# Gathers with a limit on the index: the slots of neighbouring node tiles are left out

## The chip, the cores and the metric

The kernel runs on one core of one Trainium2 chip. The time is the device time of one execution in microseconds (us), as the median of several. Before the change it is 2587.53 us, the median of 8 runs between 2582.63 and 2596.87 us.

A core has five engines with queues of their own: PE (matrix products; its weight loads are listed as PEld), DVE (vector work), ACT (activations), POOL (here above all the issuer of gathers) and SP (issuer of plain DMAs). Sixteen DMA engines move the data for all queues.

## The reference

Two graph attention layers (GAT) with normalisation and residuals, over 3,125 nodes with 768 features and 53,125 edges. The edges are 25,000 random pairs in both directions and one self loop per node, sorted by destination. The layer adds a second self loop for each node.

```python
h = relu(layernorm(x))
# layer 1: 4 heads of 256; layer 2: one head of 768
xl = (x @ W).reshape(n, heads, out_ch)
alpha_src = einsum('nhc,hc->nh', xl, a_src);  alpha_dst = einsum('nhc,hc->nh', xl, a_dst)
e = leaky_relu(alpha_src[src] + alpha_dst[dst], 0.2)
m = segment_max(e, dst);  e = exp(e - m[dst]);  s = segment_sum(e, dst)
alpha = e / (s[dst] + 1e-16)
out = segment_sum(xl[src] * alpha[:, :, None], dst) + bias
# then layer norm (layer 1 also relu), plus a dense residual of the layer's input
```

At the end `x` is added. All data are float32.

## The kernel before

The program has two parts: `in_order`, written for edges sorted by destination, and `any_order`, a general part that runs only if a flag says that the edges don't suit the first one. With these inputs only `in_order` does work.

`in_order` cuts the nodes into 25 tiles (`NB`) of 125 nodes (`P`). Since the edges are sorted, the edges of a tile lie together. For each tile the kernel takes a window of fixed size: `J` = 18 columns of 128 slots, 2,304 edges, from the first edge of the tile on (for the last tile the window is moved back so that it ends with the list). A tile has about 2,125 edges, so a window also holds edges of the neighbouring tile: at its end, or for the last tile at its beginning. A slot is column `j`, partition `p`; its number among all is `c = b * J + j`.

The stages in order of time:

1. `edge_list` (L188) reads the edge list and counts where each tile begins. `windows` (L236) loads each tile's window, turns it so that slots lie on partitions, and makes three tables of 128 x 450: `rel_s` (L259), the destination minus the tile's first node, so 0 to 124 for the tile's own edges; `idx_s` (L262), the source node as an integer, which is the row that a gather reads; and `hi_s` (L264), the source's tile. All of this is DVE work behind loads of SP. `keep` (L268) marks neighbouring slots with the same destination and is stored to memory four times by SP.
2. `softmax` (L327) for layer 1 finds the attention weight `al` of every slot with one-hot products. It works on all slots, foreign ones too, and gives them finite weights.
3. The dense product `x @ W1` (L588) writes `table1`, 3,125 rows of 1,024 floats.
4. `sums` (L460) for layer 1, the first of the two gather stages, described below. Between its columns run the steps of `end1` (normalisation and the dense product into `table2`, L655 to L683) and the dense residual (L624).
5. `softmax` and 13 of 25 residual tiles (L717) for layer 2, then `sums` for layer 2 on `table2`, with rows of 768 floats, with the rest of the residual between its columns and `end2` (L748 to L753) for the result.

In `sums`, for each tile and each column, POOL issues one indirect DMA (L477), which reads 128 rows of the table, one for each index in column `c` of `idx_s`, into a buffer `g` (10 buffers in layer 1, 13 in layer 2). DVE makes the one-hot matrix `oh` (L488) from `rel_s`: a slot whose `rel_s` lies outside 0 to 124 has a zero in all 125 columns that are used. For most columns ACT multiplies the rows with the weight into `hi`, rounded (L495), DVE forms what is left in `g` itself (L496), and PE adds both into the tile's sum `pa` (L500). For the other columns (2 of 18 in layer 1, 5 of 18 in layer 2) the weight is put into the one-hot matrix (L507, L510) and one float32 product (L512) is made. So a foreign slot's row is read, weighted and multiplied, and a zero column takes it out of the sum. Once per tile POOL gathers `ao` (L483), 128 rows of 2 or 5 floats with the weight of the self loop, which DVE compares at L518.

A gather can be issued when its buffer is free, that is when PE (and DVE) have used the buffer's last content. The order of instructions on each engine is set by a planner, which simulates the engines with a cost for each instruction and picks by the order of the program text; so POOL's place for `ao` among the gathers changes from tile to tile. Each engine then runs its queue in order.

Of the kernel before, what the change touches and what calls it, by code (L numbers as in the profile page):

```python
# [9 lines left out]
F32 = mybir.dt.float32  # L10
# [5 lines left out]
OP = mybir.AluOpType  # L16
# [10 lines left out]
J = 18  # L27
# [29 lines left out]
def in_order(  # L57
# [16 lines left out]
    nc = tc.nc  # L74
    N, D = x.shape
# [4 lines left out]
    P = 125  # L80
    NB = N // P
# [37 lines left out]
    rel_s = const.tile([128, NB * J], F32, name="rel_s")  # L119
    idx_s = const.tile([128, NB * J], I32, name="idx_s")  # L120
# [9 lines left out]
    def load_rows(q, t, src_, b):  # L130


        if b < NB - 1:
            q.dma_start(t, src_[b * P:b * P + 128, :])
        else:
            q.dma_start(t[:112], src_[b * P:b * P + 112, :])
            q.dma_start(t[112:P], src_[b * P + 112:(b + 1) * P, :])
# [29 lines left out]
    def start_of(b):  # L167
        return nc.values_load(starts[0:1, b:b + 1], engines=[SP], min_val=0, max_val=E - S)
# [67 lines left out]
    def windows(pe):  # L236

        per = 126 // J
        with tc.tile_pool(name="wn", bufs=1) as ep:
            k16 = ep.tile([NB, S], I16, name="k16")  # L240
            src_s = ep.tile([128, NB * J], F32, name="src_s")
            for b0 in range(0, NB, per):
                n = min(per, NB - b0)
                wd = ep.tile([128, 128], I32, name="wd", bufs=2)
                ws = ep.tile([128, 128], I32, name="ws", bufs=2)
                for k in range(n):
                    st = start_of(b0 + k)
                    nc.sync.dma_start(wd[k * J:(k + 1) * J, :],
                                      dst[ds(st, S)].rearrange("(j p) -> j p", p=128))
                    nc.sync.dma_start(ws[k * J:(k + 1) * J, :],  # L250
                                      src[ds(st, S)].rearrange("(j p) -> j p", p=128))
                    nc.sync.dma_start(k16[b0 + k:b0 + k + 1, :], dst16_d[ds(st, S)][None, :])
                for t, to in ((wd, dst_s), (ws, src_s)):
                    tf = ep.tile([128, 128], F32, name="tf", bufs=2)
                    nc.vector.tensor_copy(tf[:n * J, :], t[:n * J, :])
                    pt = pe.tile([128, 512], F32, name="pe")
                    nc.tensor.transpose(pt[:, :n * J], tf[:n * J, :], ident[:n * J, :n * J])
                    nc.vector.tensor_copy(to[:, b0 * J:(b0 + n) * J], pt[:, :n * J])
            nc.vector.tensor_tensor(rel_s.rearrange("p (b j) -> p b j", j=J),  # L259
                                    dst_s.rearrange("p (b j) -> p b j", j=J),  # L260
                                    base_f[:, :, None].to_broadcast([128, NB, J]), OP.subtract)
            nc.vector.tensor_copy(idx_s, src_s)  # L262
            q, _ = divided(ep, src_s, [128, NB * J], "sh")
            nc.vector.tensor_copy(hi_s, q)  # L264

            keep = ep.tile([NB, S + 2], BF16, name="keep")
            nc.vector.memset(keep, 0.0)
            nc.vector.tensor_tensor(keep[:, 1:S], k16[:, 1:], k16[:, :S - 1], OP.is_equal)  # L268
            for h in range(H):
                nc.sync.dma_start(keep_d[h * NB:(h + 1) * NB, :], keep)  # L270
# [189 lines left out]
    def sums(heads, cols, table, al, alo_d, bias, split, ahead, gp, pp, end, more=iter(())):  # L460


        width = heads * cols
        f = width // 2
        n = min(cols, f)
        todo = iter(())
        for b in range(NB):
            own = gp.tile([128, width], F32, name="own", bufs=2)
            pa = pp.tile([P, 2, 512], F32, name="pa", bufs=2)
            ao = gp.tile([128, heads + 1], F32, name="ao", bufs=2)  # L470
            for i in range(2):
                nc.tensor.matmul(pa[:, i, :f], ones_r, bias[:, i * f:(i + 1) * f], start=True, stop=False)
            for j in range(J):
                c = b * J + j
                g = gp.tile([128, width], F32R, name="g", bufs=ahead)
                gf = g.bitcast(F32)
                nc.gpsimd.indirect_dma_start(  # L477
                    out=gf, out_offset=None, in_=table[:, :],
                    in_offset=bass.IndirectOffsetOnAxis(ap=idx_s[:, c:c + 1], axis=0))
                if j == 6:  # L480
                    load_rows(nc.sync, own, table, b)
                if j == 2:
                    nc.gpsimd.indirect_dma_start(  # L483
                        out=ao, out_offset=None, in_=alo_d[:, :],
                        in_offset=bass.IndirectOffsetOnAxis(ap=at_last[:, b:b + 1], axis=0))
                if split(j) or heads > 1:
                    oh = gp.tile([128, 128], F32R, name="oh", bufs=8)
                    nc.vector.tensor_scalar(oh, iota_f, rel_s[:, c:c + 1], None, op0=OP.is_equal)  # L488
                if split(j):

                    hi = gp.tile([128, width], F32R, name="hi", bufs=4)
                    for h in range(heads):
                        cs = slice(h * cols, (h + 1) * cols)
                        a = al[:, j, h, b:b + 1]
                        nc.scalar.activation(hi[:, cs], gf[:, cs], AF.Copy, scale=a)  # L495
                        nc.vector.scalar_tensor_tensor(g[:, cs], gf[:, cs], a, hi[:, cs].bitcast(F32),  # L496
                                                       op0=OP.mult, op1=OP.subtract)
                    for t in (hi, g):
                        for i in range(2):
                            nc.tensor.matmul(pa[:, i, :f], oh[:, :P], t[:, i * f:(i + 1) * f],  # L500
                                             start=False, stop=(j == J - 1 and t is g))
                else:
                    w = gp.tile([128, heads, P], F32, name="w", bufs=4)
                    for h in range(heads):
                        a = al[:, j, h, b:b + 1]
                        if heads == 1:
                            nc.vector.tensor_scalar(w[:, h, :], iota_f[:, :P], rel_s[:, c:c + 1], a,  # L507
                                                    op0=OP.is_equal, op1=OP.mult)
                        else:
                            nc.scalar.activation(w[:, h, :], oh[:, :P].bitcast(F32), AF.Copy, scale=a)  # L510
                    for o in range(0, width, n):
                        nc.tensor.matmul(pa[:, o // f, o % f:o % f + n], w[:, o // cols, :], gf[:, o:o + n],  # L512
                                         start=False, stop=(j == J - 1 and (o + n) % f == 0))
                next(todo, None)
                next(more, None)

            iso = gp.tile([P, 1], F32, name="iso", bufs=2)
            nc.vector.tensor_tensor(iso, ao[:P, heads:], node_f[:P, b:b + 1], OP.not_equal)  # L518
            aw = gp.tile([P, heads], F32, name="aw", bufs=2)
            nc.vector.tensor_scalar(aw, ao[:P, :heads], iso, None, op0=OP.max)  # L520
            z = gp.tile([P, width], F32, name="z", bufs=2)
            for o in range(0, width, n):
                nc.vector.scalar_tensor_tensor(z[:, o:o + n], own[:P, o:o + n], aw[:, o // cols:o // cols + 1],
                                               pa[:, o // f, o % f:o % f + n], op0=OP.mult, op1=OP.add)
            for _ in todo:
                pass
            todo = end(b, z)
            next(todo)
        for _ in todo:
            pass  # L530


    with tc.tile_pool(name="m1", bufs=1) as mp:
        al1 = mp.tile([128, J, H, NB], F32, name="al1")
        with tc.tile_pool(name="w1", bufs=1) as wp, tc.tile_pool(name="pm1", bufs=1, space=PSUM) as pm1:
# [5 lines left out]
            with tc.tile_pool(name="d1", bufs=2) as dp, tc.tile_pool(name="pd1", bufs=1, space=PSUM) as pp:  # L541
# [15 lines left out]
                for _ in fold(dp, abs1, w1, NK1, H, C1, wa1, True):  # L557
                    pass
                windows(pp)
                for b in range(NB):  # L560
                    gi, o = b // GB, (b % GB) * P
# [34 lines left out]
        with tc.tile_pool(name="w2", bufs=1) as wp, tc.tile_pool(name="g1", bufs=1) as gp, \  # L596
# [53 lines left out]
            def end1(b, z):  # L650
# [33 lines left out]
                store_rows(nc.sync, table2, b, row)  # L684

            sums(H, C1, table1, al1, alo1_d, b1_r, lambda j: j % 9 != 4, 10, gp, pp, end1, later())


# [540 lines left out]
```

## Time and profile before

| | |
|---|---|
| median of 8 runs | 2587.53 us |
| profiled execution | 2584.87 us |
| its span | 2583.1 us |
| PE busy | 2271.8 us (88%) |
| DVE busy | 1889.5 us (73%) |
| ACT busy | 1311.4 us (51%) |
| POOL busy | 1300.6 us (50%) |
| moved by DMA | 638.09 MB, of which 420.88 MB by POOL's queue |
| gathers (L477) | 900, mean 1314 ns on POOL, 6.0 us from issue to landing (median) |
| TensorE clock granted | 0.938 of full speed (mean) |

The page of the profile gives the busy time of each engine over the whole span; a window query gives the same for a stretch of time. In a group's line stand the source line, the engine, the operation, the tiles written and read, the count, the busy time, the mean duration, and the idle time ahead of it with what ended it. A wait's line gives who waited for whom: total us, number of times, longest one. The busy time of a DMA instruction on POOL is the time in which POOL makes the transfer, not the transfer itself.

The stages by time: edge list and windows to about 170 us, softmax and dense product of layer 1 to about 520 us, gathers of layer 1 from about 520 to 1570 us, softmax of layer 2 and the first residual tiles to about 1900 us, gathers of layer 2 from 1791 us to the end, most of them after 1890 us.

### The profile page before, as it was taken

What the parts mean: (1) busy time and instruction counts of PE and PEld (TensorE: products, weight loads), DVE (VectorE), ACT (ScalarE), POOL (GpSimd) and SP (SyncE); (2) the same over time, 40 slices, a digit from 0 to 9 for tenths busy, and PEclk for the clock granted to TensorE, in tenths of its full rate; (3) what the DMA queues carried; (4) which work ended last, traced back from release to release, by engine and by line L of the source; (5) the groups of instructions that cost most, each with busy time, mean ns of one, the idle gap of its engine ahead of it and who ended that gap; (6) DMA issues with size and microseconds to landing.
All of it is one profiled execution on the core that took longest, in us unless ns stands there. A gap on an engine that the chain in (4) does not pass through costs nothing.

```text
span 2583.1 us, 35850 instructions
## 1 busy us (share of the span) xinstructions
PE 2271.8 (88%) x11226; PEld 1493.7 (58%) x11226; DVE 1889.5 (73%) x4289; ACT 1311.4 (51%) x2834; POOL 1300.6 (50%) x1007
## 2 busy tenths in 40 slices
PE   0969999939999999999999998768998898899776
PEld 0846654415666666666666675554566666566554
DVE  3559996026888989888898997685166777677886
ACT  5313321115887878788887995001033444444443
POOL 5100000037667667666676772002057778787775
PEclk9989999969999999999999998767999999999898
DMA  4228721176889888888888996873268998888887
GB/s 153 85 86 295 252 95 58 48 251 231 285 288 314 294 313 314 278 326 291 314 308 281 329 331 219 287 278 106 69 219 289 316 311 294 273 290 284 295 295 235
DMA packets 185428, 638.09 MB, mean 247 GB/s; under 512 B 31215, under 2 KB 50036, under 8 KB 184334
## 3 DMA queue, kind: packets, MB, share of 16 engines
q0 software_dynamic: 104032, 420.88, 47.8%
q1 hardware_dynamic: 76484, 202.08, 22.5%
q10 hardware_dynamic: 4714, 12.75, 1.4%
q8 instruction: 92, 1.51, 0.2%
q14 instruction: 106, 0.87, 0.1%
HBM read 566.11 MB, written 69.49 MB: 246 GB/s over the span
## 4 chain that ended last, share of the span: by engine, by line
PE 60%; DMA 10%; DVE 8%; issue 4%; POOL 2%; ACT 2%; SPq 1%; DVEq 0%; ACTq 0%; POOLq 0%
PE pa L500 19%; PE p L677 10%; PE pr L717 8%; PE pr L624 8%; PE pa L512 7%; DMA g<-table,idx_s 6%; PE pm L588 5%; DVE g L496 3%; DMA ao<-alo_d,at_last 2%; PE pq L377 1%; ACT hi L495 1%; POOL at L294 1%; PE p L664 1%; POOL g L477 1%; PE pr L713 1%
## 5 line engine op out<-in xcount | busy, mean ns | idle before, releaser
L477 POOL DMA_INDIRECT g<-table,idx_s x900 | 1182.8, 1314 | 1136.3 <-DVE oh L488 417.6
L495 ACT ACTIVATE hi<-g,al 128x256 fp32r<-128x256 f32 (+1 forms) x1925 | 970.7, 576 | 588.5 <-PE pa L500 281.7
L496 DVE SCALAR_TENSOR_TENSOR g<-g,al,hi 128x256 fp32r<-128x256 f32 (+1 forms) x1925 | 988.3, 566 | 116.6 <-ACT hi L495 110.9
L500 PE MATMUL pa<-hi,oh 128*125 128x512 f32 (+1 forms) x1450 | 580.0, 481 | 12.6 <-ACT hi L495 7.1
L500 PE MATMUL pa<-g,oh 128*125 128x512 f32 (+1 forms) x1450 | 457.8, 393 | 51.5 <-DVE g L496 50.4
L500 PEld LDWEIGHTS pa<-hi,oh 128*125 128x125 f32 x1450 | 269.4, 193 | 187.1 <-ACT hi L495 67.1
L500 PEld LDWEIGHTS pa<-g,oh 128*125 128x125 f32 x1450 | 268.3, 192 | 128.3 <-DVE g L496 86.5
L717 PE MATMUL pr<-wr,h 128*125 128x384 f32 x800 | 303.4, 518 | 0.0
L624 PE MATMUL pr<-h0k,wr 128*128 128x500 f32 (+1 forms) x672 | 299.0, 542 | 0.4 <-DMA h0k<-h0T_d 0.4
L677 PE MATMUL p<-w,h1T 128*125 128x384 f32 (+1 forms) x800 | 296.8, 490 | 1.8 <-DVE h1T L668 1.8
L512 PE MATMUL pa<-g,w 128*125 128x384 f32 (+1 forms) x900 | 288.8, 453 | 4.5 <-ACT w L510 3.7
L588 PE MATMUL pm<-w,h 128*125 128x512 f32 x600 | 275.5, 607 | 0.0
L512 PEld LDWEIGHTS pa<-g,w 128*125 128x125 f32 x900 | 170.3, 193 | 84.2 <-issue 25.7
L488 DVE TENSOR_SCALAR oh<-iota_f,rel_s 128x128 fp32r<-128x128 f32 x775 | 200.3, 288 | 21.1 <-PE pa L500 20.1
L717 PEld LDWEIGHTS pr<-wr,h 128*125 128x125 f32 x800 | 155.4, 199 | 94.0 <-issue 19.4
L677 PEld LDWEIGHTS p<-w,h1T 128*125 128x125 f32 x800 | 150.6, 189 | 73.5 <-issue 3.0
L588 PEld LDWEIGHTS pm<-w,h 128*125 128x125 f32 x600 | 110.0, 191 | 118.9 <-issue 118.9
L624 PEld LDWEIGHTS pr<-h0k,wr 128*128 128x128 f32 x672 | 124.2, 191 | 66.0 <-issue 22.5
L377 PE MATMUL pq<-tabs,ohs 125*128 125x100 bf16 (+1 forms) x2700 | 111.4, 199 | 42.2 <-DVE ohs L365 40.6
L377 PEld LDWEIGHTS <-ohs 125*128 125x128 bf16 x2700 | 106.2, 103 | 59.8 <-DVE ohs L365 53.1
L518 DVE TENSOR_TENSOR iso<-ao,node_f 125x1 f32<-125x1 f32 x50 | 7.8, 157 | 161.7 <-DMA ao<-alo_d,at_last 161.7
L590 ACT ACTIVATE row<-pm 125x512 f32<-125x512 f32 x50 | 29.7, 597 | 169.9 <-PE pm L588 159.8
(173 smaller groups left out, 1717.2 us busy)
## 6 DMA issues: line engine op xcount, KB each, us to landing
bd<-dst_d SPq DMA_DIRECT2D x50, 576.0 KB
bs<-slo_d SPq DMA_DIRECT2D x50, 576.0 KB
g<-table,idx_s POOLq DMA_INDIRECT x900, 6.0
r1T_d<-rt SPq DMA_DIRECT2D x100, 125.0 KB
r1t<-r1T_d SPq DMA_DIRECT2D x25, 500.0 KB
h1T_d<-h1T SPq DMA_DIRECT2D x25, 500.0 KB
h<-h1T_d SPq DMA_DIRECT2D x25, 500.0 KB
own<-table SPq DMA_DIRECT2D x24, 512.0 KB
```

What stands on the lines that cost most here:

```text
L377: nc.tensor.matmul(q[:, j], ohs[:P, (j0 + j) * 128:(j0 + j + 1) * 128], tabs[:, i], start=(i == 0), stop=(i == 2))
L477: nc.gpsimd.indirect_dma_start(out=gf, out_offset=None, in_=table[:, :], in_offset=bass.IndirectOffsetOnAxis(ap=idx_s[:, c:c + 1], axis=0))
L488: nc.vector.tensor_scalar(oh, iota_f, rel_s[:, c:c + 1], None, op0=OP.is_equal)
L495: nc.scalar.activation(hi[:, cs], gf[:, cs], AF.Copy, scale=a)
L496: nc.vector.scalar_tensor_tensor(g[:, cs], gf[:, cs], a, hi[:, cs].bitcast(F32), op0=OP.mult, op1=OP.subtract)
L500: nc.tensor.matmul(pa[:, i, :f], oh[:, :P], t[:, i * f:(i + 1) * f], start=False, stop=(j == J - 1 and t is g))
L512: nc.tensor.matmul(pa[:, o // f, o % f:o % f + n], w[:, o // cols, :], gf[:, o:o + n], start=False, stop=(j == J - 1 and (o + n) % f == 0))
L588: nc.tensor.matmul(pm, h0[gi][:, k, o:o + P], w1[:, k, i * 512:(i + 1) * 512], start=(k == 0), stop=(k == NK1 - 1))
L590: nc.scalar.activation(row[:, i * 512:(i + 1) * 512], pm, AF.Copy)
L624: nc.tensor.matmul(pm[:, :nb * P], wr1[:, k, m * 128:(m + 1) * 128], loaded[gi, k][:, :nb * P], start=(k == 0), stop=(k == NK1 - 1))
L677: nc.tensor.matmul(pm[:, :n], hT[:, k, :], w2[:, k, o:o + n], start=(k == 0), stop=(k == NK2 - 1))
L717: nc.tensor.matmul(pm[:, :384], h1[:, k, :], wr2[:, k, i * 384:(i + 1) * 384], start=False, stop=(k == NK2 - 1))
```

## The change

In `windows`, DVE marks the slots whose `rel_s` is below 0 or at least 125, except for those of tile 0 (the first 18 columns), and adds `N` = 3,125 to their index; these indices then lie past the table's last row, 3,124. In `sums`, each gather is given that last row as a limit, with the note that an index beyond it is no error (before, the instruction carried the table's 3,125 rows as its limit, and an index beyond it would have been an error): rows with such an index are not read, and their place in the buffer keeps what it held before. Tile 0 still reads every slot, and its 18 columns go through all 10 or 13 buffers, so that every buffer holds numbers from then on. What the skipped places hold is weighted and multiplied as before and meets the zero column of the one-hot matrix. The gathers of `ao` (L483) are not touched.

```diff
@@ windows
             nc.vector.tensor_tensor(rel_s.rearrange("p (b j) -> p b j", j=J),
                                     dst_s.rearrange("p (b j) -> p b j", j=J),
                                     base_f[:, :, None].to_broadcast([128, NB, J]), OP.subtract)
-            nc.vector.tensor_copy(idx_s, src_s)
+            away = ep.tile([128, NB * J], F32, name="away")
+            nc.vector.tensor_scalar(away, rel_s, 0.0, float(N), op0=OP.is_lt, op1=OP.mult)
+            past = ep.tile([128, NB * J], F32, name="past")
+            nc.vector.tensor_scalar(past, rel_s, float(P), float(N), op0=OP.is_ge, op1=OP.mult)
+            nc.vector.tensor_add(away, away, past)
+            nc.vector.memset(away[:, :J], 0.0)
+            nc.vector.tensor_add(away, away, src_s)
+            nc.vector.tensor_copy(idx_s, away)
             q, _ = divided(ep, src_s, [128, NB * J], "sh")
             nc.vector.tensor_copy(hi_s, q)
@@ sums
                 nc.gpsimd.indirect_dma_start(
                     out=gf, out_offset=None, in_=table[:, :],
-                    in_offset=bass.IndirectOffsetOnAxis(ap=idx_s[:, c:c + 1], axis=0))
+                    in_offset=bass.IndirectOffsetOnAxis(ap=idx_s[:, c:c + 1], axis=0),
+                    bounds_check=N - 1, oob_is_err=False)
```

## The prediction

> **What bounds the kernel now.** I read first the busy times of the page, then the windows by stage, then POOL's waits and its timeline in the two gather stages, and last the rows of the operations that the change touches.
>
> ```profile
> span 2583.1 us, 35850 instructions
> PE 2271.8 (88%) x11226; PEld 1493.7 (58%) x11226; DVE 1889.5 (73%) x4289; ACT 1311.4 (51%) x2834; POOL 1300.6 (50%) x1007
> DMA packets 185428, 638.09 MB, mean 247 GB/s; under 512 B 31215, under 2 KB 50036, under 8 KB 184334
> ```
>
> PE looks like the bound and POOL half idle. These are averages, so I cut the span by stage (the columns are busy us and instruction counts of PE, PE's weight loads, DVE, ACT, POOL, then PE's clock, the DMA share and GB/s):
>
> ```profile
> core 0: us, PE busy (x) PEld busy (x) DVE busy (x) ACT busy (x) POOL busy (x), PEclk, DMA share, GB/s
> 600.00:1437.00 837.00, 826.61 (x2975) 540.91 (x2975) 711.98 (x1977) 689.42 (x1751) 565.91 (x395) 0.99 0.87 300
> 1792.00:1900.00 108.00, 103.72 (x317) 58.65 (x315) 25.28 (x53) 9.97 (x11) 26.48 (x26) 0.95 0.36 119
> 1900.00:2100.00 200.00, 183.23 (x705) 130.31 (x704) 151.57 (x297) 87.83 (x101) 159.75 (x133) 0.96 0.89 303
> 2100.00:2300.00 200.00, 180.94 (x684) 126.99 (x683) 148.17 (x297) 85.04 (x99) 159.78 (x133) 0.94 0.86 289
> 2420.00:2520.00 100.00, 79.11 (x293) 52.87 (x292) 81.56 (x166) 46.68 (x54) 78.67 (x71) 0.93 0.89 301
> ```
>
> Then what POOL waits for: in layer 1 (600 to 1437 us) the first line below, in layer 2 (1900 us to the end) the second, and, of POOL's timeline in layer 2, four issues.
>
> ```profile
> POOL g L477 <- PE pa L500: 204.0, 205, 4.3
> ...
> POOL g L477 <- PE pa L500: 39.3, 129, 0.3
> ...
> 2216.53 0.94 POOL L483 DMA_INDIRECT ao<-alo_d,at_last  x1 [0.30 <-issue]
> 2217.77 0.94 POOL L477 DMA_INDIRECT g<-table,idx_s  x1 [0.30 <-issue]
> 2219.02 0.95 POOL L477 DMA_INDIRECT g<-table,idx_s  x1 [0.30 <-issue]
> 2220.27 0.94 POOL L477 DMA_INDIRECT g<-table,idx_s  x1 [0.30 <-DMA g<-table,idx_s]
> ```
>
> The reader is to see two different stages. In layer 1, PE is busy 826.6 of 837 us and POOL waits for PE to free gather buffers, up to 4.3 us at a time. POOL needs 565.9 + 395 x 0.30 (the gap ahead of every issue) = 684 us of 837, so it has 153 us over, 0.39 us per issue. In layer 2, from 1900 us on, the longest wait of POOL for anything is 0.3 us, which is the fixed gap: 159.78 + 133 x 0.30 = 199.7 us of 200. There POOL issues gathers back to back, and its pace sets the end; 450 of the layer's 475 indirect DMAs are issued that way (the 1792 to 1900 window holds about 25). PE (181 of 200 us) and the DMA engines (0.86) come next.
>
> **The change part by part.** How many rows drop out follows from the seeded edge list: a window has 2,304 slots, a node tile about 2,125 edges. In tiles 1 to 24, 4,300 slots of 55,296 are foreign. They lie at the window's end: per layer 23 gathers become wholly empty (mostly slot column 17) and 23 partly. That is 4,300 / 128 = 33.6 gathers' worth of rows, 4,300 x 4,096 B = 17.6 MB in layer 1 and 4,300 x 3,072 B = 13.2 MB in layer 2, 4.8% of the 638 MB.
>
> *New DVE work in windows().* Two compares, two adds and a memset join; the cast to integers only changes its input. The nearest rows, at the same 128x450 and lower down at another size:
>
> ```profile
> L181 DVE TENSOR_SCALAR shu<-sht 128x450 f32<-128x450 f32 x1 | 0.4, 397 | 0.0
> L182 DVE TENSOR_TENSOR shq<-shq,shu 128x450 f32<-128x450 f32 x1 | 0.6, 628 | 0.0
> L109 DVE MEMSET eps<- 128x1 f32 x1 | 0.1, 59 | 0.7 <-PEq L1215 0.7
> ```
>
> 2 x 0.40 + 2 x 0.63 + 0.06 = 2.1 us. They run once, near 162 us. Behind them on DVE stand the division that makes hi_s, the keep mask, and so SP's stores of keep and the first loads of bd behind those. DVE then idles 1.2 us for the keep store and 1.5 us for bd. If these transfers are not moved by the delay, the idle time swallows all of it; if they are, the whole softmax of layer 1 starts 2.1 us later. Ends 0 and +2.1; keep is made after the new instructions in program order, so part of it passes through: I take +1.
>
> *The gathers' bytes.* PE, DVE and ACT still work through every slot, with the buffer's old rows under a zero one-hot column, so nothing there shrinks. What shrinks is transfer time. In layer 1 it is covered by PE. In layer 2 it would be worth 13.2 MB / 0.289 MB per us = 46 us if the transfers set the pace; but POOL's issue is never held by a landing there (no wait over 0.3 us). A gather that lands earlier only makes ACT's next wait for POOL start earlier. I take 0; ends -46 and 0. The Trainium skill, in "DMA: Bandwidth & Descriptors", section "Anatomy of one DMA — SWDGE (gpsimd) path", gives a software-issued DMA a fixed part and a part that goes with bytes over 436 GB/s. By that rule the layer-2 saving would be an estimated 30 us, and the total 2558 us; the rule has no term for an issuing engine that is the bound.
>
> *POOL's time for one gather.* This is the term that decides, since 450 of them stand in a row: each 0.1 us is 45 us in layer 2, and in layer 1 only what exceeds 0.39 us counts. The rows:
>
> ```profile
> L477 POOL DMA_INDIRECT g<-table,idx_s x900 | 1182.8, 1314 | 1136.3 <-DVE oh L488 417.6 <-PE pa L500 308.4 <-DMA h<-h1T_d 221.6
> L483 POOL DMA_INDIRECT ao<-alo_d,at_last x50 | 49.7, 995 | 30.6 <-DVE iso L518 12.8 <-issue 9.8 <-DVE aw L520 4.4
> L134 POOL DMA_DIRECT2D xt<-in_x_dram x19 | 10.8, 573 | 38.9 <-DVE bn_mv L315 12.0 <-DVE bn_st L313 10.9 <-DMA ws<-in_src_dram 6.5
> ```
>
> An undisturbed gather takes 0.94 us whether its rows have 3,072 B or, for ao in layer 2, 8 B: the price goes with the instruction and its 128 indices, not with what is moved. What lies over 0.94 falls together with DVE's two-input instructions of L496. A plain DMA over 128 rows costs 0.57 us, so handling 128 indices is worth at most 0.94 - 0.57 = 0.37 us. No row has a gather with a limit that skips. Ends for an ordinary gather: 0, if the comparison is part of the price already (the gather of before already carries the table's 3,125 rows as a limit, past which an index would be an error), and +0.37, if every index is handled once more: 450 x 0.37 = +167 us. I take 0, because of that limit. Ends for a skipped row: an empty gather could cost 0.37 us less (33.6 x 0.37 = -12 us in layer 2), nothing but its gap (33.6 x 0.94 = -32 us), or 0.37 us more (+12 us). The ao row says the price doesn't follow the data, so I take 0.
>
> *The planner.* The order on each engine comes from a planner's simulated times, and five new instructions shift these by some 2 us; POOL's queue already shows it, with ao at changing places between the gathers. In layer 2 an exchange moves ao by one gather, 1.25 us, ahead of a DVE wait. I take 0, ends -5 and +5 (four such exchanges).
>
> Sum: +1 + 0 + 0 + 0. The profiled execution took 2584.87 us (span 2583.1), 2.7 us under the median of 2587.53, well inside the 2582.63 to 2596.87 of the runs; so 2586 against that execution, and 2588 to 2589 against the median. I say 2588.
>
> **The rivals.**
>
> *A: skipped rows make gathers cheaper on POOL.* For it: 23 empty gathers a layer have no row to describe, and layer 2 passes on every us. Against: 0.94 us for 8-byte rows. It gives 2588 - 12 = 2576, at most 2588 - 32 = 2556.
>
> *B, the other side: each gather pays for its limit.* Place: POOL's queue in layer 2, issue time of L477. For it: nothing covers it there, gap and busy time fill 199.7 of 200 us. Against: the table's size is already with the gather. It decides from 7.8 / 450 = 0.017 us per gather on; at 0.1 us it gives 2633, at 0.37 us 2755.
>
> *C: a gather in which rows are skipped is slower, or the planner's order falls worse.* If a skipping gather takes as much again (46 x 0.94 = 43 us in layer 2), 2631; with 0.37 us more 2605. Layer 1 hides it behind PE. Nothing in the trace speaks for it but that no row excludes it.
>
> *D: fewer bytes do pay.* For it: DMA share 0.86 to 0.89, and ACT waits 201 us for gathers in layer 2. Against: POOL never waits there. Up to 46 us: 2542; half of it 2565.
>
> **How the numbers follow.** A measurement of this kernel can tell about 0.3%, 7.8 us, from no change. Chances: forecast 0.30; A 0.22 and D 0.08, both faster; B 0.24 and C 0.16, both slower. So faster 0.30, same 0.30, slower 0.40. Two forces push from the middle: layer 2 passes on even 0.017 us per gather, and the unknown lies exactly there. The forecast's own range is 2580 to 2596. The whole range reaches down to 2560 (D with six tenths of its 46 us, A with 0.83 us less per empty gather) and up to 2650 (B with 0.14 us per gather); beyond it lie the far part of B (0.10) and the ends of D and A (0.07).
>
> **What would show it.** Right: in layer 2 POOL's gap stays 0.30, an undisturbed gather 0.94 us, the DMA share falls by some 6 points while the pace per tile (19 issues, 28.6 us) stays; in layer 1 the 40 us per tile stay. The software queue loses about 31 of its 421 MB. Wrong: a smallest gather time other than 0.94 (B), empty gathers at the end of each tile with another time (A, C), gaps over 0.30 in layer 2 (the transfers were the bound after all), or a shifted order of ao (the planner). The prediction fails above all if the price of one gather is not what I took it for.

## The result and the profile after

The changed kernel takes 2610.69 us, the median of 16 runs between 2604.94 and 2618.77. The kernel before, run beside it, takes 2587.17 us (46 runs). The ratio is 1.009, with a 95% interval from 1.0078 to 1.0103: slower by 0.9%, three times what a measurement of this kernel can tell from no change. The time lies inside the range given, but the forecast case, no change, did not come; the rival that each gather pays for its limit did, at 0.052 us per gather.

The profiled execution took 2614.92 us, 30 us over that of before and in the upper half of its runs. First the page of the kernel after: span, engines, packets, and POOL's DMA queue (packets, MB, share of the 16 engines).

```profile
span 2613.0 us, 36754 instructions
PE 2274.7 (87%) x11226; PEld 1491.9 (57%) x11226; DVE 1891.3 (72%) x4294; ACT 1309.8 (50%) x2834; POOL 1354.9 (52%) x1007
DMA packets 185436, 607.36 MB, mean 232 GB/s; under 512 B 37658, under 2 KB 56479, under 8 KB 184334
q0 software_dynamic: 104032, 390.10, 45.3%
```

PE, DVE and ACT do the same work in the same busy time to within 3 us. POOL alone has 54 us more, for the same 1,007 counted instructions. The bytes fell as planned: POOL's queue moved 390.10 MB where it had moved 420.88. Its number of packets did not fall, 104,032 in both kernels. In the trace a skipped row of layer 1, 4,096 B, is still a packet, of 4 B, which takes 9 ns where a full one takes about 188; in layer 2 two rows of 3,072 B go as one packet of 6,144 B (about 291 ns), and two skipped ones as one of 8 B (9 ns). So nothing drops out of the list that POOL makes for the DMA engines. The 904 further instructions are nearly all register moves on POOL's queue, one per gather, which take no busy time.

The windows by stage of the kernel after (columns as before: PE, weight loads, DVE, ACT, POOL, PE's clock, DMA share, GB/s):

```profile
core 0: us, PE busy (x) PEld busy (x) DVE busy (x) ACT busy (x) POOL busy (x), PEclk, DMA share, GB/s
600.00:1437.00 837.00, 824.01 (x2967) 539.09 (x2966) 710.79 (x1973) 686.94 (x1748) 585.41 (x394) 0.99 0.84 282
1792.00:1900.00 108.00, 103.66 (x319) 59.17 (x318) 24.88 (x48) 10.76 (x12) 27.25 (x24) 0.95 0.37 120
1900.00:2100.00 200.00, 175.91 (x669) 123.38 (x668) 145.29 (x289) 83.49 (x97) 161.12 (x128) 0.94 0.82 270
2100.00:2300.00 200.00, 177.27 (x667) 124.49 (x667) 145.28 (x287) 82.84 (x96) 160.85 (x129) 0.93 0.82 268
```

POOL's waits of the kernel after, first in layer 1 (600 to 1437 us), then in layer 2 (1900 us on):

```profile
POOL g L486 <- PE pa L510: 190.2, 214, 3.9
...
POOL g L486 <- issue: 53.3, 175, 0.3
POOL g L486 <- PE pa L510: 32.3, 106, 0.3
```

And POOL's timeline in layer 2 of the kernel after, five issues in a row:

```profile
2217.57 1.00 POOL L486 DMA_INDIRECT g<-table,idx_s  x1 [0.30 <-PE pa L510]
2218.87 0.99 POOL L486 DMA_INDIRECT g<-table,idx_s  x1 [0.31 <-PE pa L522]
2220.17 1.00 POOL L486 DMA_INDIRECT g<-table,idx_s  x1 [0.30 <-DVE g L506]
2221.47 1.01 POOL L486 DMA_INDIRECT g<-table,idx_s  x1 [0.30 <-issue]
2222.78 1.06 POOL L486 DMA_INDIRECT g<-table,idx_s  x1 [0.30 <-PE pa L510]
```

Layer 1 hides the dearer gathers: POOL is 19.5 us busier in that window, waits 14 us less for PE, and issues 394 gathers in place of 395. The layer's last gather is issued at 1567.7 us, before at 1568.0. In layer 2 there is no room. The second 200 us window gives 160.85 + 129 x 0.30 = 199.6 us for POOL, so it still issues back to back, but 129 instructions where there were 133. The gap is the old 0.30; the gather is 1.00 where it was 0.94. The DMA engines became emptier (0.82 after 0.86) and PE too, which shows that neither is what holds POOL.

From the first gather of the layer's tile 1 to its last, the stretch is 700.5 us (1893.8 to 2594.4), before 669.9 (1895.2 to 2565.1): 30.6 us, as much as the whole spans differ (29.9). The line of the gathers alone, from 1900 to 2500 us, gives smallest, median and largest duration in ns. Before:

```profile
L477 POOL DMA_INDIRECT g<-table,idx_s x384: 942/948/3139, 1899.9 to 2498.8; - x192
```

After:

```profile
L486 POOL DMA_INDIRECT g<-table,idx_s x370: 994/1008/3857, 1898.5 to 2498.9; - x185
```

The smallest went from 942 to 994 ns. Over 450 gathers in a row that is 450 x 0.052 = 23.4 us, against 23.5 us between the medians. That the two agree to 0.1 us is luck: the four kernels below with the limit alone, or with the change in layer 2 alone, lose 14 to 19 us between medians, and the stretch of layer 2 varies by some 9 us between profiled executions whose gathers there carry no limit (669.9 us before, 668.6 with only the DVE work, 677.8 with the limit in layer 1 alone).

### The profile page after: what moved, and what is told of

Its sections match the earlier page's. It is cut to its first block, busy times and chain, and to the rows that moved or that the text cites. A ratio compares the mean times of both kernels' runs of the same rounds, so it can differ in the third digit from the quotient of the medians.

```text
span 2613.0 us, 36754 instructions
## 1 busy us (share of the span) xinstructions
PE 2274.7 (87%) x11226; PEld 1491.9 (57%) x11226; DVE 1891.3 (72%) x4294; ACT 1309.8 (50%) x2834; POOL 1354.9 (52%) x1007
## 3 DMA queue, kind: packets, MB, share of 16 engines
q0 software_dynamic: 104032, 390.10, 45.3%
## 5 line engine op out<-in xcount | busy, mean ns | idle before, releaser
L486 POOL DMA_INDIRECT g<-table,idx_s x900 | 1233.9, 1371 | 1114.9 <-DVE oh L498 415.2
```

The lines of the kernel that those rows point to most:

```text
L486: nc.gpsimd.indirect_dma_start(out=gf, out_offset=None, in_=table[:, :], in_offset=bass.IndirectOffsetOnAxis(ap=idx_s[:, c:c + 1], axis=0) ...
```

## The experiments

**Only the limit.** The kernel before, and one argument more; nothing is skipped.

```diff
-                    in_offset=bass.IndirectOffsetOnAxis(ap=idx_s[:, c:c + 1], axis=0))
+                    in_offset=bass.IndirectOffsetOnAxis(ap=idx_s[:, c:c + 1], axis=0),
+                    bounds_check=N - 1, oob_is_err=False)
```

> Before, with the limit given to every gather and the indices left alone: no row is skipped, no DVE work is added, the order on every engine is that of before. Theory P (the price of the limit): each gather costs POOL 52 ns more whether it skips or not, layer 2 passes 450 of them on: 2587 + 23 to 30 = 2610 to 2617 us; smallest gather 994 ns, bytes of the software queue unchanged at 420.9 MB. Rival S (the gathers that skip rows are the slow ones): 2587 us, since none skips. Rival V (the new DVE work and the order that follows from it): 2587 us.

Measured: 2604.87 us, ratio 1.0068 (1.0044 to 1.0091). The page and the gathers' line in layer 2 of this kernel:

```profile
span 2610.1 us, 36750 instructions
q0 software_dynamic: 104032, 420.88, 47.5%
L477 POOL DMA_INDIRECT g<-table,idx_s x375: 994/1002/3845, 1899.7 to 2499.6; - x188
```

All bytes are moved, exactly 900 instructions are new, and the smallest gather is 994 ns. So the limit alone, with no row skipped and the instructions of each engine in the old order, brings most of the loss: 18.6 us between medians. That is 5 us under the range expected; its interval overlaps that of the full change.

**Only the DVE work.** The five new DVE operations with their marks multiplied by 0, and no limit.

```diff
-            nc.vector.tensor_scalar(away, rel_s, 0.0, float(N), op0=OP.is_lt, op1=OP.mult)
+            nc.vector.tensor_scalar(away, rel_s, 0.0, 0.0, op0=OP.is_lt, op1=OP.mult)
...
-                    in_offset=bass.IndirectOffsetOnAxis(ap=idx_s[:, c:c + 1], axis=0),
-                    bounds_check=N - 1, oob_is_err=False)
+                    in_offset=bass.IndirectOffsetOnAxis(ap=idx_s[:, c:c + 1], axis=0))
```

> After, without the limit, and with both marks multiplied by 0 in place of the table's size, so that the indices stay what they were: only the five new DVE instructions remain. P: 2587 to 2589 us, gathers at 942 ns. V: 2605 to 2613 us. S: 2587 us.

Measured: 2586.08 us, ratio 0.9999 (0.9982 to 1.0016), smallest gather 942 ns. The DVE work costs nothing that can be told.

**One layer at a time.** The changed kernel with the limit and the skipping in one layer; the other layer gathers by a second table of plain indices, `idx_p`. For layer 1 (the other is its mirror image):

```diff
+            nc.vector.tensor_copy(idx_p, src_s)
...
-                    in_offset=bass.IndirectOffsetOnAxis(ap=idx_s[:, c:c + 1], axis=0),
-                    bounds_check=N - 1, oob_is_err=False)
+                    in_offset=bass.IndirectOffsetOnAxis(ap=(idx_s if heads > 1 else idx_p)[:, c:c + 1], axis=0),
+                    **(dict(bounds_check=N - 1, oob_is_err=False) if heads > 1 else {}))
```

> The limit and the skipped rows in layer 1 alone; layer 2 reads by a second table with the plain indices and without a limit (one more DVE cast). P: layer 1 has 0.39 us per issue to spare on POOL, so its 450 dearer gathers cost nothing: 2587 to 2590 us, with 17.6 MB fewer. V: 2605 us or more. If bytes paid in layer 1 it would be under 2580 us.

> The limit and the left-out slots in layer 2 only; layer 1 gathers with a plain second table of indices and no limit. P (every limited gather costs POOL about 0.05 us more, and only layer 2, where POOL issues without a break, passes it on): layer 2 as in the changed kernel, smallest gather 0.995 us, layer 1 smallest gather as before; 432 to 450 x 0.052 = 22 to 23 us, time 2605 to 2612, the whole of the change's loss. Rival (part of the loss comes from layer 1 or from the DVE work): less than 2602.

Measured: layer 1 alone 2590.63 us, ratio 1.0021 (1.0001 to 1.0040); layer 2 alone 2605.25 us, ratio 1.0076 (1.0051 to 1.0101). In layer 2 the gathers of the first kernel have 942 ns as their smallest and those of the second 994. So most of the loss comes from layer 2, by the same addition per gather. What layer 1 adds, 0.2% or 4.4 us between medians and 0.6 us above the range expected, is at the edge of what can be told from nothing. The trace does not show it in layer 1, whose last gather is issued at 1569.2 us in that run, 1 us later than before; what that execution has more lies in layer 2, where its gathers are those of before (677.8 us for the stretch above, in place of 669.9).

**A layer 2 that reads nothing.** The kernel with the limit in layer 2 alone, and there every slot of tiles 1 to 24 marked as past the end. It leaves out reading these rows, so its output is not the reference's.

```diff
+            nc.vector.memset(away, float(N))
             nc.vector.memset(away[:, :J], 0.0)
```

> The limit in layer 2 alone, and there every slot of tiles 1 to 24 has an index past the end: 432 gathers of layer 2 read no row at all (the output is computed from tile 0's rows, so this part of the computation is left out), layer 1 as before. P: POOL still issues 450 gathers back to back, each at 994 ns undisturbed: 2610 to 2617 us, although some 159 MB are not moved. Rival D (transfers set the pace of layer 2): well under 2587 us, to 2500 us, PE being the next bound at 0.9 busy. S: skipped rows make each gather slower still: over 2640 us; if a skipped row were cheaper to issue than a read one: under 2600 us.

Measured: 2586.64 us, ratio 1.0005 (0.9985 to 1.0025). Windows, queue and gathers' line of this kernel:

```profile
1900.00:2100.00 200.00, 182.35 (x702) 131.34 (x701) 153.57 (x304) 88.76 (x102) 159.45 (x134) 0.93 0.20 55
2100.00:2300.00 200.00, 180.26 (x689) 129.49 (x687) 147.37 (x295) 85.40 (x98) 158.84 (x136) 0.93 0.17 45
...
q0 software_dynamic: 104032, 251.24, 28.9%
L489 POOL DMA_INDIRECT g<-table,idx_s x385: 994/1017/3140, 1899.2 to 2499.1; - x193
```

This missed both theories. The part that was to be tested held: a gather that reads no row at all still takes POOL 994 ns, and POOL still fills 158.84 + 136 x 0.30 = 199.6 of 200 us, with the DMA engines at 0.17. But the time fell by 18.6 us against the kernel with the limit in layer 2 alone, so traffic is not quite free on POOL either. To see where, I sorted the 432 gathers of layer 2's tiles 1 to 24 in the trace by whether any of DVE's SCALAR_TENSOR_TENSOR operations (those that write `g` and `z`, each with two tensors as inputs) ran during them:

```
                          none ran: number, mean ns     some ran: number, mean ns     sum of all, us
before                           68,   947                   364, 1229                  511.6
after                            83,  1004                   349, 1310                  540.5
limit in layer 2 alone           79,  1000                   353, 1287                  533.3
layer 2 reads nothing            60,  1008                   372, 1213                  511.9
```

A gather that is left alone takes 947 ns without a limit and 1000 to 1008 with one, with traffic or without. A gather that meets DVE takes longer, and this excess is what shrinks without traffic: from 287 to 205 ns over the others. In the eleven traces with traffic, one for each other kernel of this document, the excess lies between 260 and 306 ns. Not every such operation counts. Of the gathers of before, 28 met only L523, whose second input is PE's sum `pa` in place of a buffer: they took 947 ns, as if alone, though L523 ran during 0.51 us of each in the mean. Of the 266 that met only L496 (inputs `g` and `hi`), the 62 whose meeting lasted 0.3 to 0.6 us took 1035 ns. Why traffic makes these meetings dearer no run shows. The Trainium skill, in "GPSIMD Engine Reference", section "Specifications", says that GpSimd and VectorE share their access to the on-chip buffer and contend when a DVE instruction has two inputs there; the 947 against 1229 ns of before, and L523 against L496, agree with that. In "Perfetto Trace Analysis", section "DMA Instruction — SWDGE (GPSIMD)", it says that the profile's interval for such a DMA ends when the last descriptor is written, not when the data have moved; the 994 ns of a gather without data, with its packets all there, agree with that too.

**What in the limit costs.** Two variants of the kernel with only the limit: the limit loaded into a register of POOL once per layer, and the limit with an index beyond it as an error, as it was without the argument.

```diff
+        last = nc.values_load(lim[0:1, 0:1], engines=[mybir.EngineType.Pool], min_val=1, max_val=N - 1)
...
-                    bounds_check=N - 1, oob_is_err=False)
+                    bounds_check=last, oob_is_err=False)
```

> As the first experiment (limit on every gather, no row skipped), but the limit is loaded once per layer from a tile into a register, and the 900 register moves ahead of the gathers go. P: the price lies in the gather itself, which has an operand more to take care of: smallest gather 994 ns, 2610 to 2617 us. Rival M (the register move ahead of each gather is the price): 942 ns, 2587 us.

```diff
-                    bounds_check=N - 1, oob_is_err=False)
+                    bounds_check=N - 1, oob_is_err=True)
```

> As the first experiment, but an index past the limit is an error, as in the kernel before, and not left out. If the price comes with the limit as such: 2610 to 2617 us and 994 ns. If it comes with leaving out without an error: 2587 us and 942 ns.

Measured: with the register 2602.55 us, ratio 1.0058 (1.0040 to 1.0076). The page's span and the gathers' line:

```profile
span 2600.7 us, 35878 instructions
L480 POOL DMA_INDIRECT g<-table,idx_s x372: 994/1002/3842, 1899.6 to 2499.2; - x186
```

With the error 2606.47 us, ratio 1.0078 (1.0047 to 1.0108), and this line:

```profile
L477 POOL DMA_INDIRECT g<-table,idx_s x369: 1007/1017/3849, 1899.9 to 2499.6; - x185
```

Both times lie below the range expected, by 7 and 4 us, and the 1007 ns were not expected. Without the 900 register moves the smallest gather is still 994 ns, so the moves are not the price. With the error it is 1007, so leaving rows out isn't either. The price belongs to a gather that is given a limit; what POOL does in these 52 ns no run shows.

**The limit only where it is needed.** The changed kernel with limit and marks only in columns 15 to 17 of tiles 1 to 23.

```diff
+            nc.vector.memset(away.rearrange("p (b j) -> p b j", j=J)[:, :, :15], 0.0)
+            nc.vector.memset(away[:, (NB - 1) * J:], 0.0)
...
-                    bounds_check=N - 1, oob_is_err=False)
+                    **(dict(bounds_check=N - 1, oob_is_err=False) if j >= 15 and 0 < b < NB - 1 else {}))
```

> The changed kernel with the limit, and the left-out slots, only where nearly all foreign slots lie: columns 15 to 17 of tiles 1 to 23, 69 of the 450 gathers of a layer; the other 381 carry plain indices and no limit. P (the price is paid by each gather that carries a limit): 69 x 0.052 = 3.6 us in layer 2, so the limited ones at 0.995 us at least and the others at 0.945; time 2587 to 2593. Rival (the price belongs to the program as a whole, once any gather has a limit): all gathers at 0.995, 2605 to 2612. Rival (bytes pay once the price is small: some 12 of 13.2 MB less are still left out in layer 2): up to 40 us, 2545 to 2580.

Measured: 2593.86 us, ratio 1.0021 (1.0006 to 1.0037), 0.9 us above the range expected. In the trace the 363 gathers of layer 2's tiles 1 to 24 without a limit have 942 ns as their smallest and 1153 as their mean (before 1159), so each gather pays for itself. The 69 with a limit start at 994, but their mean is 1478, where the same slots had 1315 before: beside the 69 x 0.052 = 3.6 us there are 7.6 us more in all, and the others took 2 us less. These 7.6 us can't be put down to the limit: the same 69 slots have a mean of 1329 in the changed kernel, with a limit on each, and 1411 with the limit in layer 1 alone, with none. Nearly all of the bytes are saved here (391.40 MB moved), at a seventh of the price, and still nothing is won.

**Fewer issues on POOL.** If POOL's pace sets the end of layer 2, taking instructions from it must pay. The kernel before gathers `ao` once per tile; here all 25 are gathered during tile 0, where POOL has idle time, into buffers of their own.

```diff
+        aos = [gp.tile([128, heads + 1], F32, name="ao", bufs=NB) for _ in range(NB)]
...
-                if j == 2:
-                    nc.gpsimd.indirect_dma_start(
-                        out=ao, out_offset=None, in_=alo_d[:, :],
-                        in_offset=bass.IndirectOffsetOnAxis(ap=at_last[:, b:b + 1], axis=0))
+                if b == 0 and j == ahead - 1:
+                    for t in range(NB):
+                        nc.gpsimd.indirect_dma_start(
+                            out=aos[t], out_offset=None, in_=alo_d[:, :],
+                            in_offset=bass.IndirectOffsetOnAxis(ap=at_last[:, t:t + 1], axis=0))
```

> Before, with one edit: all 25 gathers of ao are issued in tile 0, after the gathers that fill the buffers (25 small buffers in place of 2). POOL sits idle there for 27 and 45 us in layer 2. If POOL's issue sets the end of layer 2, this takes about 21 issues of 0.95 + 0.30 us from the stretch without gaps: 2587 - 26 = 2561 us. Rival D (transfers set the pace): 2587 us, since the bytes are the same. Rival W (PE's or DVE's waits would take over at once): between 2575 and 2587 us.

The same edit on the changed kernel:

> The same edit made to the kernel after. P: the price of the limit stays on top: 2561 + 23 to 30 = 2584 to 2591 us. If with the shorter queue something else than POOL sets layer 2, the limit costs less: under 2580 us; if the fewer bytes then pay, at or under the time of the same edit without the limit.

Measured: 2551.58 us on the kernel before, ratio 0.9858 (0.9830 to 0.9887), and 2576.9 us on the changed one, ratio 0.9955 (0.9934 to 0.9975). The first beats both kernels; its windows in layer 2:

```profile
1900.00:2100.00 200.00, 188.62 (x732) 132.61 (x731) 159.46 (x316) 92.18 (x106) 159.27 (x134) 0.97 0.91 319
2100.00:2300.00 200.00, 184.87 (x715) 129.86 (x714) 156.58 (x315) 90.69 (x104) 159.77 (x133) 0.97 0.90 306
```

POOL's windows are as full as before, 133 and 134 issues, but now all of them are gathers of `g`. The same bytes as before move faster, 306 GB/s where it was 289, which shows once more that the transfers did not set the pace before. The gain is 10 us more than expected, and the traces show where. From the first gather of tile 1 to the last, layer 2 takes 642.6 us where it took 669.9: 27 us less, close to the 26 expected. Layer 1 takes 932.0 us where it took 942.3, for which the expectation had nothing. There POOL has time over, but DVE's idle time for `ao` went from 99.0 us to 0.7 in that layer; that this is the reason is likely, not shown. On the changed kernel 2576.9 us lies under the range expected, and even under the 2580 set as the sign that something else than POOL then bounds layer 2. But the time it was to be added to had come out 9.4 us lower than forecast: between the two kernels the change costs 25.3 us here, inside the 23 to 30, with POOL's list shorter by the `ao` gathers in both, and about the 23.5 us that it costs without this edit.

## Why the prediction was right or wrong

*What bounds each stage: right.* Layer 1 took 450 dearer gathers and ended at the same time; layer 2 passed them on, and gave back 27 us when 21 issues were taken out of its row.

*POOL's time for one gather: this is the step that failed.* It read "I take 0, because of that limit", on the ground that the gather of before already carries the table's 3,125 rows. That size is carried, but it is not what a limit costs: with the argument a gather takes 0.052 us more, even where nothing is skipped and even where an index beyond it is an error. The bounds of 0 and +0.37 us held the value, and rival B named place, sign and the point from which it decides; its worked examples, 0.1 and 0.37 us, were too large. Over all 432 gathers of tiles 1 to 24 the mean went from 1184 to 1251 ns, and the sum, 28.9 us, is nearly the 30.6 by which the stretch grew. Of these 67 ns 52 are the limit's. The other 15 lie mostly in meetings with DVE and can't be called the change's: with the limit on every gather and nothing skipped the mean is 1231, and with the limit in layer 1 alone, none in this layer, 1203.

*Skipped rows at 0: right, and rival A fell.* A gather without any row to read costs POOL the same 994 ns, and the number of packets does not fall. Rival C fell as well: in the changed kernel gathers that skip and those that don't have the same smallest time, and with nothing skipped most of the loss is there. What is left for it is little: the 46 skipping gathers of layer 2 grew by 99 ns (empty) and 130 (partly empty) in the mean and the others by 61, some 2.5 us in all. The same slots' means differ by as much where nothing is skipped or limited in that layer (1195 and 1254 before, 1299 and 1386 with the limit in layer 1 alone), and the intervals of 1.0068 and 1.009 overlap.

*The bytes at 0: right for this change, but not as a rule.* 13.2 MB fewer in layer 2 bought nothing to be seen: the limit in layer 2 alone takes 2605.25 us, the limit everywhere without skipping 2604.87. But 156 MB fewer bought 18.6 us. By proportion 13.2 MB are worth 1.6 us. The step's reason, that POOL never waits for a landing, was true; that traffic then can't matter at all did not follow. The estimate by the Trainium skill's rule in "DMA: Bandwidth & Descriptors", section "Anatomy of one DMA — SWDGE (gpsimd) path", 30 us saved and 2558 us in all, is not borne out.

*DVE work at +1: right within what can be told.* The five operations took the 2.1 us that their rows gave (0.38, 0.38, 0.62, 0.61 and 0.07), and alone they moved the time by nothing that can be measured. DVE's idle time for the keep store fell from 1.2 to 0.4 us, so part of the cover named is seen at work.

*The planner at 0: right.* POOL, PE and ACT run their instructions in the order of before; DVE has the added lines, and SP alone has some early loads and a store at other places.

## What to carry to other kernels

Before an argument is added to an instruction that is issued in a row without a break, its price per issue decides, and an instruction which "has something like it already" is no row for it: time one with and one without. Rows left out of a gather by their index save bytes, not issue time, since they stay in the list as small packets. Where one queue's issue sets the pace, look first for issues that can go elsewhere in time: moving the 25 small gathers of each layer out of the row gave 36.9 us, some 27 of them in the layer whose pace POOL sets, and leaving out 5% of the bytes gave nothing.

## What the hardware showed that was not expected

- A limit on the index costs POOL 52 ns per gather of 128 rows (942 to 994), 65 ns if a breach is an error (1007); loading it into a register beforehand saves none of that.
- A skipped row of 4,096 B is a packet of 4 B for 9 ns, two skipped rows of 3,072 B are one of 8 B; a gather in which all 128 are skipped takes POOL as long, when undisturbed, as one in which none is (994 ns at least).
- Traffic on the DMA engines does not change a gather that POOL makes undisturbed (1000 ns with it, 1008 without), but one that meets DVE's two-input operations is longer with it: 1269 to 1310 ns in the mean in the five traces with this limit in layer 2's gathers and the traffic, 1213 without it.
- Of DVE's two-input operations, the one whose second input is PE's sum (L523) does not lengthen a gather that it meets (947 ns); the one with both inputs in buffers (L496) does (1035 ns for a meeting of 0.3 to 0.6 us).
